# A fifth score buffer in a two-layer graph network: queries wait in DRAM, and U2 takes U1's place

## The chip, the cores and the metric

The kernel runs on one core of a Trainium2 chip. A core has a matrix engine (TensorE, PE in the profile, with its weight loads as PEld), three engines for elementwise work (VectorE or DVE, ScalarE or ACT, GpSimd or POOL), and SyncE (SP), which in this kernel issues nearly all DMA transfers. Each engine takes its instructions in the order in which the program has them and waits where one isn't ready. The metric is the device time of one execution in microseconds.

## The reference

A layer of graph diffusion with a sparsified attention is followed by a graph attention layer; N = 3327 nodes, 256 features. Cut to what is computed:

```python
h = relu(layernorm(x))
# layer 0: two steps
R = adj + I;  R = R / R.sum(-1)
Z = 0; Xf = Xa = h
for n in range(2):
    q = Xa @ W1.T @ W2.T                  # (N, 64)
    k = Xa @ W3.T                         # (N, 64)
    A = softmax(q @ k.T)                  # (N, N)
    A = A where it is in the row's smallest set that sums to 0.9, else 0
    A = A / A.sum(-1)
    Xf = R @ Xf
    Xa = A @ Xa
    Z = Z + Xf @ U1[n].T + Xa @ U2[n].T
x = x + layernorm(h + Z)
# layer 1: four heads of 64
h = relu(layernorm(x)); hp = h @ W
s, d = hp . a_src, hp . a_dst             # per node and head
P = softmax over j of leaky_relu(s_i + d_j, 0.2) where adj > 0
x = x + elu(P @ hp)
```

Everything is float32. The output is x.

## The kernel before

Nodes are cut into 26 row tiles of 128 (the last has 127). The whole work is one function, `fast`; another, `general`, takes over only for data on which a guess in it fails.

**A plan sets the order.** The class `Plan` collects pieces of work. Each is put with an engine (or two that it may choose between), an estimated length, a rank, the pieces that it needs, a lag after which others may count on it, and the buffers that it takes and gives back, by name. `Plan.order` then simulates a list schedule with these figures: whenever an engine is free, it takes the piece of lowest rank whose needs and buffers are there. The result is a fixed order on each engine, which `Plan.issue` writes out. The figures thus set the order, not the times. Buffers are named there with counts, e.g. four `e`, four `at`, two `pl`, three `et`.

**The start.** Each tile of x is normalised, turned, and projected with `wqk` to a 128-row `kq`, with the key in one half of the partitions and the query in the other (`prepare`, L1212). GpSimd copies the key into `kt`, which holds all keys, and the query into `qq`, which holds all queries (26 x 128 floats in each partition); SP copies the query into the other half of `qq` (`double`, L1246), since the key tiles are spread over both halves[...]. `project_u` (L1263) multiplies each tile with U1 of both steps at once; R is applied to these products afterwards. U1 is in a buffer called `late`, U2 in one of its own; both come in at the start (U2 at 15 us, L584 in the trace). After `project_u`, `late` is used for the weights of layer 1.

**A row tile of a step** (class `Row`):

- logits (L898): PE multiplies the tile's queries with all keys, into 3327 columns, four parts of up to 1024 columns; ACT copies each part to `e`, with the exponential (L913). `e` has 128 x 3328 floats, and there are four such buffers.
- the search for the threshold at which the kept set sums to 0.9: a first guess from the mean and variance of the row's logits (`stats`, L809, from the queries and a sum over the keys, `gk`), counts on ACT (L950), windows and maxima on DVE (L1006, L1011), sorting and choosing on DVE and POOL.
- drop (L1064): DVE sets to zero what is under the threshold, in four parts.
- the turn of the kept probabilities, as PE needs them with columns on partitions. In step 0, three of the four parts go without PE: DVE transposes small blocks in place (`turn_blocks`, L1100), SP writes them to DRAM (`put_blocks`, L1104) and fetches them back in the right order, in four transfers a part (`get_blocks`, L1108); `attend_blocks` (L1118) multiplies them with the features from `e` itself, and only then the buffer is free. The last part, and in step 1 all of them, are turned by PE (L1077) and copied to `et` (L1088); `attend` (L1095).

**Beside it** goes R times the features (class `Full`, L1142): the adjacency is streamed from DRAM in transfers of four tiles (`at`, L1136, seven for a row tile). PE puts such rows between the pieces of the attention.

**The end of a row tile of step 0** (`finish1`, L1280): the attended features are turned, projected to the next step's `kq` (L1299), and multiplied with U2. Before the last logits of step 0, `kt` and `qq` still hold that step's keys and queries; so the new key and query go to DRAM (`spread`, L1311: the key to `kts`, the query to both halves of `qqs`, three transfers); for the last three tiles, which come after those logits, directly to `kt` and `qq`. `fetch_keys` and `fetch_queries` bring them back in two and three large transfers at the turn of the steps. `finish2` (L1376) ends a row of step 1: layer norm, residual and the projections for layer 1.

**Layer 1** (`attend_neighbours`, L1598) runs in four blocks of columns; four of its large tiles lie where the `e` buffers were.

Three parts of the order matter here. All of SP's transfers share one queue of issue: loads of adjacency, puts, gets, the spread of keys and queries, stores. The planner puts row tiles' logits as early as an `e` is free. And the statistics of a step come in three groups of row tiles (0 to 2, 3 to 12, 13 to 25).

Of the kernel before, what the change touches and what calls it, by code (L numbers as in the profile page):

```python
# [19 lines left out]
P = 128  # L20
# [567 lines left out]
def fast(  # L588
# [31 lines left out]
    kts = spill.tile([P, NT * P], F32, name="kts")  # L620
    qqs = spill.tile([P, NT, P], F32, name="qqs")
# [26 lines left out]
    with ExitStack() as l0:  # L648
# [17 lines left out]
        qq = wpool.tile([P, NT, P], F32, name="qq")  # L666

# [5 lines left out]
        u2 = wpool.tile([P, 2, 2 * D], F32, name="u2")  # L673
# [3 lines left out]
        gk = wpool.tile([P, 2 * DA + 1], F32, name="gk")  # L677
        GP.memset(gk, 0.0)
        GP.tensor_copy(gk[:DA, DA + 1 :], ident[:DA, :DA])
# [22 lines left out]
        def weights():  # L702
# [10 lines left out]
            for n in range(STEPS):  # L713
                cols = slice((1 - n) * D, (2 - n) * D)
                uloads.append(
                    plan.put(
                        "SP", 0.4, -196.5 + n, nc.sync.dma_start, u1[:, :, cols],
                        u1t[n].rearrange("(c p) o -> p c o", p=P), lag=8.0,
                    )
                )  # L720
                plan.put(
                    "SP", 0.4, -150.0, nc.sync.dma_start, u2[:, :, cols], u2t[n].rearrange("(c p) o -> p c o", p=P)
                )
# [25 lines left out]

        def layer1_loads():  # L750
# [24 lines left out]
        def moments(t, kq, ps_k, ps_g):  # L775
# [4 lines left out]
            held = {}  # L780
# [28 lines left out]
        def stats(lo, hi, rank, needs, scaled):  # L809
# [6 lines left out]
            def product(held, t0, m):  # L816

                held["ps"] = ps_x.tile([P, 3, 2 * DA + 1], F32, name="px")
                for k in range(m):
                    T.matmul(held["ps"][:, k, :], qq[:, t0 + k, :], gk, start=True, stop=True)  # L820
# [6 lines left out]
            def square(held, t0, m):  # L827
                qg = held["qg"]
                for k in range(m):
                    junk = small.tile([P, DA], F32, name="qj", bufs=1)  # L830
                    V.scalar_tensor_tensor(
                        junk, qg[:, k, :DA], 1.0, qg[:, k, DA + 1 :], ALU.mult, ALU.mult,
                        accum_out=stat[:, 0, t0 + k : t0 + k + 1],
                    )
                V.tensor_copy(stat[:, 1, t0 : t0 + m], qg[:, :m, DA])

            for t0 in range(lo, hi, 3):
                held, m = {}, min(3, hi - t0)
# [24 lines left out]
            return plan.put("DVE", 0.6, rank, rest, needs=[a])  # L863

        plan = Plan(dict(rows=1, mvs=3, pl=2, px=2, acca=1, accf=1, et=3, at=4, y=1, e2=3, mask=2, **BUFS))

        class Row:
# [10 lines left out]
            def open(self):  # L878
                self.e = epool.tile([P, NP], F32, name="e")
# [6 lines left out]
            def logits(self, k):  # L886
# [7 lines left out]
                for r in range(2):  # L894
# [5 lines left out]
                        qq[half, self.i, :],  # L900
# [223 lines left out]
        JC = 4  # L1124

# [52 lines left out]
        def keys_summed(t, kq, ps_k, ps_g, rank, needs, tags, give):  # L1178
            turn, copy, product, gather = moments(t, kq, ps_k, ps_g)
# [32 lines left out]
        def prepare(t, measured):  # L1212
# [28 lines left out]
            def keys():  # L1241
                GP.tensor_copy(kt[mine, cols], held["kq"][mine])
                GP.tensor_copy(qq[other, t, :], held["kq"][other])

            def double():
                nc.sync.dma_start(qq[mine, t, :], held["kq"][other])  # L1246
# [7 lines left out]
            k = plan.put("POOL", 0.7, r, keys, needs=[a])  # L1254
            q = plan.put("SP", 0.2, r, double, needs=[a])
            g = t % 4 == 0 and keys_summed(
                t, lambda: held["kq"], lambda: ps_a.tile([P, P], F32, name="acca"),
# [3 lines left out]
            return [k, q], g  # L1261
# [18 lines left out]
        def finish1(row, done, rank):  # L1280
# [27 lines left out]
            def queries():  # L1308
                GP.tensor_copy(qq[other, t, :], held["kq"][other])

            def spread():  # L1311
                kq = held["kq"]
                if not direct:
                    nc.sync.dma_start(kts[mine, cols], kq[mine])
                    nc.sync.dma_start(qqs[other, t, :], kq[other])
                nc.sync.dma_start((qq if direct else qqs)[mine, t, :], kq[other])

            def project_u2():
                ps = held["pu"] = ps_x.tile([P, 2 * D], F32, name="px")
                for k in range(2):  # L1320
                    T.matmul(ps, held["xt"][:, k, :], u2[:, k, :], start=(k == 0), stop=(k == 1))
# [23 lines left out]
            kq = [a]  # L1345
            if direct:
                kq = [
                    plan.put("DVE", 0.2, r, keys, needs=[a, drawn[0]]),
                    plan.put("POOL", 0.4, r, queries, needs=[a, drawn[0]]),
                ]  # L1350
            kq.append(plan.put("SP", 0.3, r, spread, needs=[a, drawn[0] if direct else None]))
            g = t % 4 == 0 and keys_summed(
                t, lambda: held["kq"], lambda: ps_x.tile([P, P], F32, name="px"),
                lambda: ps_x.tile([P, DA + 1], F32, name="px"), r, [a, guessed[0]], ("px", "px"), [],
            ) or None
            plan.put("SP", 0.02, r, lambda: None, needs=[kq, g], give=["kq"], lag=0.0)
            a = plan.put("PE", 1.75, r + 0.1, project_u2, needs=[x_], take=["px"])
            a = plan.put("ACT", 0.56, r + 0.1, stage, needs=[a], take=["ystage"], give=["px", "xt"])
            a = plan.put("POOL", 0.8, r + 0.3, add, needs=[a])
            y = plan.put("SP", 0.1, r + 0.3, store, needs=[a], give=["ystage"], lag=3.0)  # L1360
            return kq, g, y

        def fetch_keys(r):
            half = slice(r * DA, r * DA + DA)
            w = max(half_of(t)[2].stop for t in range(LAST + 1) if side(t) == r)
            nc.sync.dma_start(kt[half, :w], kts[half, :w])

        def fetch_queries(lo, hi):
            nc.sync.dma_start(qq[:, lo:hi, :], qqs[:, lo:hi, :])
# [6 lines left out]
        def finish2(row, done, z, rank):  # L1376
# [64 lines left out]
            x_ = plan.put("SP", 0.1, r - 1.5, fetch, needs=[row.pieces["guess"]], take=["ystage"], lag=3.0)  # L1441
# [4 lines left out]
            s_ = plan.put("SP", 0.1, r, store, needs=[a])  # L1446
# [35 lines left out]
        def search(row, rank, keys, stats_of, fresh):  # L1482
# [4 lines left out]
            for g in range(2):  # L1487

                def logits(g=g):
# [4 lines left out]
                    "PE", 1.95 - 0.67 * g, rank - 2.5, logits, needs=[keys, fresh, a], take=["pl", "pl"] + ["e", "sc"] * (1 - g)  # L1494
# [37 lines left out]
        GROUPS = -(-NT // 4)  # L1532

        def attention(row, rank, total, drops, right):
            a = None
            if row.i < BLOCKED[row.n]:
                come = []
                for g in range(3):
                    b = plan.put("DVE", 1.25, rank - 1.001, row.turn_blocks, g, needs=[drops[g]])
                    b = plan.put("SP", 0.5, rank - 1.0, row.put_blocks, g, needs=[b], lag=3.5)  # L1540
                    b = plan.put("POOL", 0.02, -90.0, lambda: None, needs=[b], lag=0.0)
                    come.append(
                        [plan.put("SP", 0.45, rank - 1.0, row.get_blocks, g, o, needs=[b], lag=3.5) for o in range(4)]
# [6 lines left out]
                for j in (0, 4, 8, 12, 24, 16, 20):  # L1550
                    if j == 24:
# [4 lines left out]
                        take=["acca"] * (j == 0), give=["e"] * (j == 20),  # L1556
                    )
                return plan.put("ACT", 0.4, rank - 2.7, row.attended, needs=[a, total], take=["xa"], give=["acca", "sc"])
            for g in range(GROUPS):
# [4 lines left out]
                    give=["e"] * (g == GROUPS - 1),  # L1564
# [10 lines left out]
        def full(n, t, rank, right, after):  # L1575
# [3 lines left out]
                plan.put("SP", 0.1, rank, f.load, q, needs=[after], take=["at"], lag=3.3) for q in range(-(-NT // JC))  # L1579
# [13 lines left out]
            if n == 1:  # L1593
                b = plan.put("SP", 0.1, rank, f.fetch, needs=[loads[-1], stored[t]], take=["base"], lag=3.0)
# [3 lines left out]
        def attend_neighbours(rows, ends, done, fulls):  # L1598
# [29 lines left out]
            opened = [plan.put("SP", 0.02, 59.0, open_heads, needs=[logits_done, counted], lag=0.0)]  # L1628
# [48 lines left out]
            for b in range(4):  # L1677
# [14 lines left out]
                for j in range(NT):  # L1692
# [83 lines left out]
                    else:  # L1776
                        loads = [
                            plan.put("SP", 0.1, rank, load, g, needs=[logits_done], take=["at"], lag=4.0)
# [138 lines left out]
        late, hs, turned_h, drawn, guessed, loaded, stored = {}, [[None] * NT], [None] * NT, [None], [None], [None], [None] * NT  # L1917
# [24 lines left out]
        keys, sums = [a for a, _ in parts], [b for _, b in parts]  # L1942
        layer1_ready = None
        sources = [project_u(t, -1.9 + 0.001 * t) for t in range(NT)]
        right, fresh, failed, queries = None, None, [], [None] * NT
        for n in range(STEPS):
# [3 lines left out]
                lambda: V.tensor_scalar(gk[:, : DA + 1], gk[:, : DA + 1], 1.0 / (-(-NT // 4) * P), None, ALU.mult), needs=[sums],  # L1950
            )
            cuts = (0, 3, NT // 2, NT)
            of = {}
            for k in range(3):
                p = stats(
                    cuts[k], cuts[k + 1], base + (-50.0, -2.35, 0.0)[k], [keys, queries[cuts[k] : cuts[k + 1]], fresh],
                    scaled,
                )
                of.update(dict.fromkeys(range(cuts[k], cuts[k + 1]), p))
            if n == 0:  # L1960
                guessed[0] = [*{id(p): p for p in of.values()}.values()]
            rows = [Row(n, i) for i in range(NT)]
            found = [search(r, base + r.i, [keys, queries[r.i]], of[r.i], fresh) for r in rows]
# [8 lines left out]
            if n == 0:  # L1972
                ends = [finish1(r, done[r.i], base + r.i + 0.2) for r in rows]
                stored = [y for _, _, y in ends]

                keys, queries, after = [k for k, _, _ in ends], [k for k, _, _ in ends], [drawn[0]]
                for fn, args, rest in (
                    (fetch_keys, (0,), ends[: LAST + 1]), (fetch_keys, (1,), ends[: LAST + 1]),
                    *((fetch_queries, (lo, min(lo + 8, LAST + 1)), ends[lo : lo + 8]) for lo in range(0, LAST + 1, 8)),
                ):  # L1980
                    p = plan.put("SP", 0.1, base + NT, fn, *args, needs=[after, [k for k, _, _ in rest]], lag=5.0)
                    if fn is fetch_keys:
                        keys.append(p)
                    else:
                        for t in range(*args):
                            queries[t] = [queries[t], p]
                    after = [plan.put("POOL", 0.02, -90.0, lambda: None, needs=[p], lag=0.0)]
                sums = [g for _, g, _ in ends]
# [14 lines left out]
                a = plan.put("SP", 0.5, base + 4.0, layer1, needs=[used, done[3]], take=["et"], lag=8.0)  # L2003
# [79 lines left out]
```

## Time and profile before

| | |
|---|---|
| median of 3 runs | 2159.17 us (2158.55 to 2160.39) |
| the profiled execution | 2158.39 us |
| its span | 2156.6 us |
| granted TensorE clock | 0.995 |
| PE busy | 2098.1 us (97%) |
| weight loads busy | 1464.1 us (68%) |
| DVE busy | 1757.0 us (81%) |
| ACT busy | 1324.9 us (61%) |
| POOL busy | 945.9 us (44%) |
| data moved | 265.5 MB, 123 GB/s on average |

The stages in the trace: the start to about 100 us, step 0 to about 850, step 1 to about 1600, layer 1 to the end. The profile is one execution, so its times differ a little from the median. A line of the table of waits has the engine and what it was to do, what it waited for, then the microseconds in total, the number of waits and the longest. In the timeline a line begins with its start and its length in us; in brackets is the idle time before it and what ended it.

### The profile page before, as it was taken

Reading aid. Unit: us, or ns where it says so; the run is one execution under the profiler, and the core shown is the slowest. Engines: PE = TensorE matmul, PEld = TensorE weight load, DVE = VectorE, ACT = ScalarE, POOL = GpSimd, SP = SyncE. Lnnn points to the kernel's source line nnn. Section 1 sums busy time; section 2 is a strip of 40 time slices with the busy share of each in tenths; the row PEclk is TensorE's granted clock in tenths of the full one; section 3 lists DMA queues with packets and bytes.
Section 4 is the critical chain, followed back from the end, with each engine's and each line's share of the span. In section 5 each row is a group of like instructions: output and inputs, shape, how many; then the busy total and the mean of one; then the engine's idle time right before and its main releaser. Section 6 shows DMA issues by size and latency. Waiting matters only on the chain. (4 is left out here: it accounts for less than half of the span.)

```text
span 2156.6 us, 35324 instructions
## 1 busy us (share of the span) xinstructions
PE 2098.1 (97%) x11247; PEld 1464.1 (68%) x11247; DVE 1757.0 (81%) x4436; ACT 1324.9 (61%) x2444; POOL 945.9 (44%) x2259
## 2 busy tenths in 40 slices
PE   8999999999999999999999999999999999999997
PEld 6577777777777777778877888888888433333332
DVE  5579887878777781578999899978878999989895
ACT  4677565665456621687777767777773556565552
POOL 5367555555554630367667666567553100000001
PEclk9999999999999999999999999999999999999999
DMA  4077777777776796522222222222224545354441
GB/s 122 22 172 186 184 181 177 177 177 173 187 173 162 154 240 181 150 62 76 65 64 59 62 62 62 74 76 75 68 70 134 153 128 160 114 153 117 117 124 33
DMA packets 398243, 265.52 MB, mean 123 GB/s; under 512 B 181370, under 2 KB 352096, under 8 KB 398048
## 3 DMA queue, kind: packets, MB, share of 16 engines
q1 hardware_dynamic: 397152, 262.97, 47.1%
q8 instruction: 91, 1.49, 0.3%
q14 instruction: 104, 0.85, 0.1%
q10 hardware_dynamic: 896, 0.21, 0.0%
HBM read 205.31 MB, written 56.84 MB: 122 GB/s over the span
## 5 line engine op out<-in xcount | busy, mean ns | idle before, releaser
L950 ACT ACTIVATE junk<-e,sc 128x3327 fp8e5<-128x3327 f32 x182 | 558.2, 3067 | 65.2 <-POOL sc L995 64.0
L1095 PE MATMUL acca<-rhs,et 128*128 128x256 f32 x1456 | 336.4, 379 | 0.0
L1142 PE MATMUL accf<-main,at 128*128 128x257 f32 x1352 | 314.0, 383 | 8.3 <-DMA at<-in_adjt_dram 6.6
L1142 PE MATMUL accf<-c,at 128*128 128x256 f32 x1352 | 313.4, 382 | 3.5 <-DVE f L1154 2.5
L1118 PE MATMUL acca<-rhs,e 128*128 128x256 f32 x1248 | 284.6, 383 | 22.3 <-DMA e<-blocks 21.5
L1095 PEld LDWEIGHTS acca<-rhs,et 128*128 128x128 f32 x1456 | 268.9, 190 | 32.3
L1142 PEld LDWEIGHTS accf<-main,at 128*128 128x128 f32 x1352 | 252.0, 190 | 57.0 <-issue 10.9
L1142 PEld LDWEIGHTS accf<-c,at 128*128 128x128 f32 x1352 | 249.8, 190 | 49.1 <-issue 9.7
L1118 PEld LDWEIGHTS acca<-rhs,e 128*128 128x128 f32 x1248 | 243.8, 197 | 57.5 <-issue 23.6
L1006 DVE SCALAR_TENSOR_TENSOR y<-e,sc 128x1639 f32<-128x1639 f32 x104 | 208.6, 2006 | 58.2 <-POOL sc L992 55.9
L1011 DVE MAX8 cands<-y 128x8 f32<-128x205 f32 (+1 forms) x832 | 243.0, 362 | 3.6
L913 ACT ACTIVATE e<-pl 128x1024 f32<-128x1024 f32 x208 | 183.7, 889 | 68.4 <-PE pl L898 66.2
L1064 DVE SCALAR_TENSOR_TENSOR e<-e,thr 128x1024 f32<-128x1024 f32 x208 | 219.0, 1075 | 4.8 <-DVE thr L1059 2.8
L1888 POOL TENSOR_TENSOR qq<-qq 128x256 f32<-128x256 f32 x4 | 3.0, 756 | 446.3 <-ACT qq L1884 446.2
L1722 ACT ACTIVATE et<-at 128x448 bf16<-128x448 f32 (+1 forms) x204 | 112.2, 550 | 130.1 <-DVE e L1733 75.1
L1749 PE MATMUL pl<-e,main 128*64 128x416 f32 x1024 | 188.8, 516 | 0.0
L898 PE MATMUL pl<-kt,qq 64*128 64x512 f32 (+1 forms) x832 | 173.6, 535 | 0.0
L1749 PEld LDWEIGHTS pl<-e,main 128*64 128x64 f32 x1024 | 70.0, 137 | 109.4 <-issue 92.3
L1733 DVE SCALAR_TENSOR_TENSOR e<-c,low,et 128x832 f32<-128x832 f32 x128 | 128.9, 1072 | 6.3 <-issue 3.2
L898 PEld LDWEIGHTS pl<-kt,qq 64*128 64x128 f32 x832 | 71.5, 186 | 83.8 <-issue 75.7
L1721 ACT ACTIVATE at<-at 128x448 f32<-128x448 f32 (+1 forms) x204 | 110.5, 542 | 26.2 <-DMA at<-in_adjt_dram 26.2
L1088 ACT COPY et<-px 128x512 f32<-128x512 f32 (+1 forms) x129 | 67.3, 533 | 95.1 <-PE px L1077 47.8
(546 smaller groups left out, 3408.8 us busy)
## 6 DMA issues: line engine op xcount, KB each, us to landing
at<-in_adjt_dram SPq DMA_DIRECT2D x414, 256.0 KB
blocks<-e SPq DMA_DIRECT2D x78, 512.0 KB
e<-blocks SPq DMA_DIRECT2D x312, 128.0 KB
at<-in_adjt_dram SPq DMA_DIRECT2D x102, 192.0 KB
at<-in_adjt_dram SPq DMA_DIRECT2D x52, 128.0 KB
ys<-ystage SPq DMA_DIRECT2D x26, 256.0 KB
rhs<-in_x_dram SPq DMA_DIRECT2D x26, 128.0 KB
ystage<-in_x_dram SPq DMA_DIRECT2D x26, 128.0 KB
```

The source lines that it names most:

```text
L898: T.matmul(pl[:, lo : lo + m], qq[half, self.i, :], kt[half, 512 * k : 512 * k + m], start=True, stop=True,)
L913: S.activation(to, pl, AF.Exp, accum_out=(self.p0, self.p1, self.p2, self.p3)[k],)
L950: S.activation(junk[:, :N], self.e[:, :N], fn, bias=t, scale=-1.0, accum_out=dst, saturate=False)
L1006: V.scalar_tensor_tensor(self.y[:, : hi - lo], self.e[:, lo:hi], self.up, self.e[:, lo:hi], ALU.is_lt, ALU.mult, accum_out=(self.h0, self. ...
L1011: V.max(self.cands[:, a * PIECES // 2 + k, :], self.y[:, at[k] - lo : at[k + 1] - lo])
L1064: V.scalar_tensor_tensor(piece, piece, self.thr[:, o : o + 1], piece, ALU.is_gt, ALU.mult)
L1095: T.matmul(self.acc, et[:, j - 4 * g, :], rhs[self.n][:, j, :], start=(j == 0), stop=j == NT - 1 and self.i >= BLOCKED[self.n],)
L1118: T.matmul(self.acc, lhs, rhs[self.n][:, j, :], start=(j == 0), stop=stop and j == js[-1])
L1142: T.matmul(self.acc[:, : self.w], self.at[j // JC][:, j % JC, :], self.src[:, j, : self.w], start=(j == 0), stop=(j == NT - 1),)
L1722: S.activation(to, src, AF.Sign)
L1733: V.scalar_tensor_tensor(held["e"][:, k, :], extra["both"][b % 2][:, k, :], low[:, j, k : k + 1], held["mask"], ALU.max, ALU.mult,)
L1749: T.matmul(q["acc"][a][k * FH : (k + 1) * FH, c, :C], main[:, j, h * FH : (h + 1) * FH], held["e"][:, h, c * C : (c + 1) * C], start=(j == 0),
```

## The change

A fifth buffer for `e` is made from the place of `qq`. Of a step's row tiles every fifth (2, 7, 12, 17, 22 in step 0; 1, 6, 11, 16, 21 in step 1) uses it, as `own_e` says; the others share the four.

- *Queries.* They wait in DRAM (`kqs`, one for each step) and come to the chip for four row tiles at a time, into `qg`, of which there are two. Step 0's first eight tiles go there directly, the others by `fetch_queries`: two transfers of 64x512, four small ones for the last group. A group's fetch waits until the logits and statistics that used its buffer are done.
- *Keys and queries of the next step.* `spread` is one transfer of 128x128 for a row tile, `kq` as it is, in place of three. The keys come back in six transfers (64x512 or 64x384) in place of two. GpSimd's copies of queries remain for the first eight tiles alone; the last three tiles of step 0 send their query through DRAM too.
- *U2* is loaded into U1's buffer after the last `project_u`. The weights of layer 1, which take that buffer next, are loaded after the last U2 product has been stored, at the turn of the steps, and layer 1's score products follow there; before, they came at about 220 to 250 us.
- *Statistics* come in groups of four row tiles, in pieces of two instead of three; each step has its own `gk`, so that the next step's key sums needn't wait for this step's statistics.
- *The planner's figures*: lengths of SP's issues go from 0.1 to 0.4 us or so, the lag of a put from 3.5 to 6.0, that of a get from 3.5 to 4.5.

Which matmuls there are isn't changed. The diff, cut:

```diff
-        kts = spill.tile([P, NT * P], F32, name="kts")
-        qqs = spill.tile([P, NT, P], F32, name="qqs")
+        kqs = [spill.tile([P, NT, P], F32, name=f"kqs{n}") for n in range(STEPS)]
...
-        qq = wpool.tile([P, NT, P], F32, name="qq")
...
-        u2 = wpool.tile([P, 2, 2 * D], F32, name="u2")
...
-        gk = wpool.tile([P, 2 * DA + 1], F32, name="gk")
+        gks = [wpool.tile([P, 2 * DA + 1], F32, name=f"gk{n}") for n in range(STEPS)]
...
-                plan.put(
-                    "SP", 0.4, -150.0, nc.sync.dma_start, u2[:, :, cols], u2t[n].rearrange("(c p) o -> p c o", p=P)
-                )
...
+        def u2_loads():
+            late["u2"] = wpool.tile([P, 2, 2 * D], F32, name="late")
+            for n in range(STEPS):
+                nc.sync.dma_start(
+                    late["u2"][:, :, (1 - n) * D : (2 - n) * D], u2t[n].rearrange("(c p) o -> p c o", p=P)
+                )
...
-            for t0 in range(lo, hi, 3):
-                held, m = {}, min(3, hi - t0)
+            for t0 in range(lo, hi, 2):
+                held, m = {}, min(2, hi - t0)
...
+        own_e = [[("e", "e5")[i % 5 == 2 - n] for i in range(NT)] for n in range(STEPS)]
...
-                self.e = epool.tile([P, NP], F32, name="e")
+                if own_e[self.n][self.i] == "e":
+                    self.e = epool.tile([P, NP], F32, name="e")
+                else:
+                    self.e = wpool.tile([P, NP], F32, name="qq")
...
-                GP.tensor_copy(qq[other, t, :], held["kq"][other])
+                if t < 8:
+                    if t % 4 == 0:
+                        qg[0, t // 4] = small.tile([P, 4, P], F32, name="qg", bufs=2)
+                    GP.tensor_copy(qg[0, t // 4][other, t % 4, :], held["kq"][other])
 
             def double():
-                nc.sync.dma_start(qq[mine, t, :], held["kq"][other])
+                to = qg[0, t // 4][mine, t % 4, :] if t < 8 else kqs[0][other, t, :]
+                nc.sync.dma_start(to, held["kq"][other])
...
+        def fetch_queries(n, g):
+            lo, hi = 4 * g, min(4 * g + 4, NT)
+            to = qg[n, g] = small.tile([P, 4, P], F32, name="qg", bufs=2)
+            for t0, t1 in ((lo, hi),) if g < 6 else ((24, 25), (25, 26)):
+                other = half_of(t0)[1]
+                for r in range(2):
+                    nc.sync.dma_start(to[r * DA : r * DA + DA, t0 - lo : t1 - lo, :], kqs[n][other, t0:t1, :])
...
             def spread():
-                kq = held["kq"]
-                if not direct:
-                    nc.sync.dma_start(kts[mine, cols], kq[mine])
-                    nc.sync.dma_start(qqs[other, t, :], kq[other])
-                nc.sync.dma_start((qq if direct else qqs)[mine, t, :], kq[other])
+                nc.sync.dma_start(kqs[1][:, t, :], held["kq"])
...
-                    b = plan.put("SP", 0.5, rank - 1.0, row.put_blocks, g, needs=[b], lag=3.5)
+                    b = plan.put("SP", 0.5, rank - 1.0, row.put_blocks, g, needs=[b], lag=6.0)
...
-                        [plan.put("SP", 0.45, rank - 1.0, row.get_blocks, g, o, needs=[b], lag=3.5) for o in range(4)]
+                        [plan.put("SP", 0.6, rank - 1.0, row.get_blocks, g, o, needs=[b], lag=4.5) for o in range(4)]
...
-                plan.put("SP", 0.1, rank, f.load, q, needs=[after], take=["at"], lag=3.3) for q in range(-(-NT // JC))
+                plan.put("SP", 0.4, rank, f.load, q, needs=[after], take=["at"], lag=3.3) for q in range(-(-NT // JC))
...
+        u2_loaded = plan.put("SP", 0.9, -1.7, u2_loads, needs=sources, lag=5.0)
...
-            cuts = (0, 3, NT // 2, NT)
...
+            for g in range(GROUPS):
+                lo, hi = 4 * g, min(4 * g + 4, NT)
+                r = base + lo - 6.0
+                if n == 0 and g < 2:
+                    q = saved[lo:hi]
+                else:
+                    q = plan.put(
+                        "SP", 1.2, r, fetch_queries, n, g, needs=[saved[lo:hi], all_saved if n == 0 else None], take=["qg"], lag=3.0
+                    )
+                known, read = stats(n, lo, hi, base - 50.0 if g == 0 else r, [keys, q, fresh], scaled)
+                found += [search(rows[t], base + t, [keys, q], known, fresh) for t in range(lo, hi)]
...
-                a = plan.put("SP", 0.5, base + 4.0, layer1, needs=[used, done[3]], take=["et"], lag=8.0)
+                a = plan.put("SP", 1.8, base + NT + 1.0, layer1, needs=[used, stored], take=["et"], lag=8.0)
```

## The prediction

> **What bounds the kernel now.** I read the page's busy times first, then TensorE's waits, then the engines by stretch, then the timeline around the longest wait.
>
> ```profile
> PE 2098.1 (97%) x11247; PEld 1464.1 (68%) x11247; DVE 1757.0 (81%) x4436; ACT 1324.9 (61%) x2444; POOL 945.9 (44%) x2259
> ```
>
> TensorE (PE) works 2098.1 of the span's 2156.6 us, so 58.5 us are all that a new order can win. The table of stretches (columns: length, then PE, weight loads, DVE, ACT and POOL busy, granted clock, DMA share, GB/s) says where they lie:
>
> ```profile
> 0.00:60.00 60.00, 50.91 (x286) 37.99 (x287) 30.24 (x121) 30.43 (x83) 32.00 (x111) 0.94 0.39 111
> 60.00:100.00 40.00, 39.98 (x117) 17.98 (x116) 21.80 (x83) 25.46 (x60) 14.00 (x40) 1.00 0.00 1
> 100.00:850.00 750.00, 718.38 (x3285) 567.06 (x3285) 575.80 (x1526) 427.15 (x723) 400.28 (x956) 1.00 0.76 179
> 850.00:1600.00 750.00, 745.20 (x3769) 604.03 (x3766) 629.54 (x2011) 550.64 (x911) 458.88 (x1072) 1.00 0.27 76
> 1600.00:2157.00 557.00, 543.66 (x3801) 237.03 (x3799) 499.65 (x698) 291.20 (x670) 40.72 (x82) 0.99 0.41 121
> ```
>
> Idle PE: 9.1 us at the head, 31.6 in step 0 (100 to 850 us), 4.8 in step 1, 13.3 after, of which some 12 are the tail after the last matmul. Step 0 holds more than half, and TensorE's waits name its cause:
>
> ```profile
> PE acca L1118 <- DMA e<-blocks: 21.5, 16, 3.1
> PE accf L1142 <- DMA at<-in_adjt_dram: 6.6, 5, 2.9
> PE px L1233 <- ACT kq L1239: 4.2, 2, 3.1
> ```
>
> Here the first product of a row tile's attention (L1118) waits for the gathers of that row's transposed blocks (21.5 us in 16 waits). The longest one in the timeline:
>
> ```profile
> 227.74 2.51 SPq L1111 DMA_DIRECT2D e<-blocks  x4
> ...
> 229.82 1.03 PE L1095 MATMUL acca<-rhs,et 128*128 128x256 f32 x4
> 233.91 3.73 PE L1118 MATMUL acca<-rhs,e 128*128 128x256 f32 x16 [3.06 <-DMA e<-blocks]
> ```
>
> The last gather is issued by 230.25 and PE goes on 3.7 us later, so the row itself is late. From a step-0 row's first logits (L898) to its first L1118 the shortest chains of the trace take 66 us (row 0 66.1, row 21 66.0, row 19 66.3, row 20 66.7). Between those two points the order puts other PE work; multiplying each instruction by its duration in the trace (0.432 us a 128x256 pair, 3.35 us a row's logits, 1.72 us a U2 product), that is 71.8 us on average, and the rows that wait are those with 62 to 68.
>
> **What the Trainium skill says.** "Perfetto Trace Analysis", Optimization Strategy: consistent bubbles can mean that there isn't room for the next tile, i.e. too few buffers. The trace agrees in part: a row of step 0 takes PE about 28.7 us (750 over 26), four e buffers thus span 115 us, and the chain (66), the attention and the waiting in between have to fit in them. "DMA: Bandwidth & Descriptors", Anatomy of one DMA: a transfer costs some 2 us whatever its size, mostly its completion, and a semaphore wait stands on the issuing sequencer before dispatch. The trace agrees: the 3.7 us above, for 128 KB. It also means that a load which waits holds up whatever is behind it on SP. Same page, Issuing engines are not separate DMA queues: small transfers are bound by their descriptors. The trace has 181370 of 398243 packets under 512 bytes, mostly these gathers; their number doesn't change.
>
> **The change part by part**, against the profiled execution's 2158.39 us (1.8 outside the span; the median of the runs is 0.8 higher, which I add at the end). No matmul is added or removed; in the changed program PE has the same instructions in another order. So everything is idle time.
>
> 1. *Fifth e buffer and the new planner lags in step 0.* Counted the same way in the changed order, 83.8 us of PE work lie between a row's first logits and its first L1118, 12 more than before. The rows at or under the 66 us chain are 0 (62.6), 1 (64.7), 12 (64.5) and 13 (65.9); the next are 14 (70.6) and 20 (71.2). Row 12 waits about 1.7, row 13 about 0.3, row 1 nothing, as row 0's wait comes in between. About 2 more for chains that run longer than the shortest. With row 0 (next step, 4.1) some 8 of 21.5 us remain: **-13.4**.
> 2. *U2's load.* Before, U1 and U2 were both on chip by 16 us. Now U2 goes into U1's buffer, so its two loads wait on SP for the last `project_u`, and the first adjacency loads stand behind them. Those were fetched far ahead:
>
> ```profile
> 49.41 2.00 SPq L1136 DMA_DIRECT2D at<-in_adjt_dram  x4
> ```
>
>    That cover is gone: two issues at 0.47 us, one of 0.5, then 768 KB at the 330 GB/s of those four loads (1 MB from 50.8 to 54.0 us; 2.3 us for 768 KB) and completion, about 4 us; PE has 2.0 us of logits to do meanwhile, so it stops for some 2 us (1.5 to 4) near 100 us. The same time counts for row 0's chain: its turn stands 53.4 us of PE work after its logits, and took 57.0. Both together cost 4.1 us in place of 1.55, which is in step 1's remainder.
> 3. *The head.* U2's two loads (0.94 us of SP, 512 KB, 1.6 us at 330 GB/s) no longer stand in front of the queries' copies at 15.2 us. PE's stop of 3.13 us before 21.18 is on that path: **-1.7** (0 to -2.5).
> 4. *Step 0 to step 1.* The first row of step 1 has its turn 60.5 us of PE work after its first logits (64.7 before). Before, that chain took 65.0 us, 2.9 of it behind statistics on DVE that now come elsewhere: 62.1, so **+1.5** (0 to 5). The next have 66, 76 and 75.5. Layer 1's score products (eight DVE operations of 0.42 us at 247 us) move here, where DVE waits for rows anyway; its cost without that cover is 3.4. The keys' fetch, six transfers instead of two, is 2 us of SP; row 24, the first behind it, has 81.7 us for its 66.
> 5. *Fewer transfers, more of others.* A row's key and query leave in one issue instead of three (0.46 to 0.93 us each), 46 fewer; 22 fetches of queries and keys come in place of 5. SP's issues for a row were 12 x 0.51, 3 x 0.39, 7 x 0.33 and about 2 more, 11.5 of 28.7 us: not a bound. 0 on the path, and a little for the gathers behind them. The fetches wait on SP for logits that are four or more rows old: 0, if those are done by then.
> 6. *Statistics in seven groups instead of three*: four more times seven small DVE operations a step (L844 to L858, 0.17 us each) and three more copies (L835, 0.17), 5.3 us a step. DVE works 575.8 of 750 and 629.5 of 750: hidden, but where it stands in a chain it shows: **+1** (0 to 3).
> 7. Adjacency waits (6.6 us), step 1's other rows (PE work from logits to turn 84.6 before, 85.5 after, none under 73), layer 1 and the tail: unchanged, **0** (-6 to +8 for the adjacency loads, which share SP's queue with a new order).
>
> Sum: -13.4 - 1.7 + 1.5 + 1 = -12.6; 2158.4 - 12.6 + 0.8 = 2146.6, about 2147.
>
> **Rivals.**
> *More is won.* If the 4 idle us of row 0 overlap and the new order also ends the adjacency waits and the rest of the row waits, -21.5 + 4.1 - 1.7 - 6.6 = -25.7: 2133. For it: those waits come from the same queue, now less loaded. Against: they are five single events (at 302, 331, 566, 762 and 798 us), and the puts and gathers that they share SP with all stay.
> *The place is taken.* The longer distance is used up: chains get longer because an earlier row means more rows in flight on DVE and ACT, or because a put waits on SP for its transposition. The mean real chain was already 76, against the shortest of 66; if it went to 84 to 88, the waits come back to 18 or so: about 2156. Against: DVE and ACT are at 77% and 57% in step 0, and a row may sit ready without harm.
> *Slower: adjacency loads behind waiting puts.* SP keeps its order. Puts and gathers now stand further ahead of their use, so SP may wait for DVE's transpositions while adjacency loads stand behind them with only four buffers' lead (16 matmuls, 7 us). At 0.9 us of late loads for each of 26 rows, +23, the result is -12.6 + 23 = +10: 2170. It turns the sign from 0.5 us a row (12.6 / 26), and reaches the slower side from 0.65. For it: five such waits exist already, up to 2.9 us. Against: they were 0.25 us a row.
>
> **How the numbers follow.** Chances: the forecast 0.50, more won 0.20, place taken 0.15, slower 0.15. A difference under 0.2% (4.3 us) is about what a measurement of this kernel can't tell from none. The forecast and the first rival lie below 2154.9; of the place taken a fifth does, the rest is the same: faster 0.73, same 0.12, slower 0.15. For 8 in 10 the range goes from 2136 (the sum with steps 1, 3 and 7 at their good ends) to 2164 (place taken whole and the beginning of the slower case); the forecast's own range is 2140 to 2153.
>
> **What would show it.** Right: waits of L1118 for blocks of 5 to 10 us in all, among them row 0, 12 and 13; PE idle 15 to 24 us between 100 and 850 us instead of 31.6; a stop near 100 us before the first L1142; a gap of under 2 us where 3.13 stood; a first turn of step 1 late by 0 to 3. Wrong: waits of L1118 of 15 us or more with longer chains (place taken), L1142 waiting for `at` over 20 us (slower), or more than 5 us of new idle time in step 1, where I see nothing change.

## The result, and the profile after

The kernel after takes 2145.39 us (median of 4 runs, 2141.34 to 2147.9), the kernel before 2159.12 us (median of 4, run with it); the ratio is 0.9934, 95% interval 0.9917 to 0.9951. The forecast was 2147 with a range of 2136 to 2164.

The profiled execution took 2146.1 us, its span is 2144.3 us. First the page's busy times and the table of stretches of the kernel after (columns as before):

```profile
PE 2096.3 (98%) x11247; PEld 1467.9 (68%) x11247; DVE 1763.6 (82%) x4510; ACT 1319.7 (62%) x2446; POOL 960.8 (45%) x2248
```

```profile
0.00:60.00 60.00, 52.12 (x282) 37.33 (x283) 30.53 (x116) 29.40 (x81) 26.32 (x95) 0.94 0.31 84
60.00:100.00 40.00, 35.76 (x100) 15.40 (x99) 19.11 (x66) 27.66 (x62) 14.67 (x39) 1.00 0.12 38
100.00:850.00 750.00, 739.14 (x3400) 587.87 (x3399) 581.93 (x1595) 427.87 (x740) 420.27 (x961) 0.99 0.79 184
850.00:1600.00 750.00, 740.87 (x3753) 603.55 (x3752) 647.29 (x2086) 559.10 (x917) 475.40 (x1113) 1.00 0.26 73
```

PE's idle time went from 58.5 to 48.0 us (2144.3 - 2096.3). By stretch: head 9.1 to 7.9, 60 to 100 us nothing to 4.2, step 0 from 31.6 to 10.9, step 1 from 4.8 to 9.1; what is left, after 1600 us, from 12.9 to 15.9. So step 0 won 20.7 us, and the change lost about half of that again elsewhere. TensorE's waits, from the top of the kernel after's answer and then the two lines on the blocks (those rows whose e lies in the fifth buffer read `qq`):

```profile
PE accf L1150 <- DMA at<-in_adjt_dram: 8.3, 3, 3.8
PE accf L1150 <- DVE f L1162: 4.2, 3, 1.7
PE accf L1150 <- ACT f L1157: 3.9, 3, 3.3
...
PE acca L1125 <- DMA qq<-blocks: 0.8, 2, 0.5
...
PE acca L1125 <- DMA e<-blocks: 0.3, 1, 0.3
```

The waits for blocks fell from 21.5 us to 1.1. The largest stops now are others. In the timeline of the kernel after, the first is U2's, the second comes with layer 1's weights, which SP issues after the first fetch of features and ahead of the next adjacency loads:

```profile
99.66 8.00 PE L1150 MATMUL accf<-main,at 128*128 128x257 f32 x28 [3.84 <-DMA at<-in_adjt_dram]
```

```profile
814.12 0.43 SPq L1383 DMA_DIRECT2D rhs<-ys  x1
814.59 0.68 SPq L757 DMA_DIRECT2D late<-in_ln_g_dram  x1
815.32 0.48 SPq L758 DMA_DIRECT2D late<-in_ln_b_dram  x1
815.84 0.43 SPq L759 DMA_DIRECT2D et<-in_gat_a_dram  x1
816.31 0.43 SPq L760 DMA_DIRECT2D late<-in_gat_w_dram  x1
816.84 4.15 SPq L1144 DMA_DIRECT2D at<-in_adjt_dram  x4
```

```profile
781.91 0.41 PE L1084 MATMUL px<-ident,e 128*128 128x128 f32 x2 [2.09 <-DVE bad L1474]
...
824.26 4.45 PE L1150 MATMUL accf<-main,at 128*128 128x257 f32 x12 [3.62 <-DMA at<-in_adjt_dram]
...
933.83 2.50 PE L1150 MATMUL accf<-c,at 128*128 128x256 f32 x5 [3.25 <-ACT f L1157]
```

### The profile page after: what moved, and what is told of

It is laid out like the page before. It is cut to its first block, busy times and chain, and to the rows that moved or that the text cites. A ratio compares the mean times of both kernels' runs of the same rounds, so it can differ in the third digit from the quotient of the medians.

```text
span 2144.3 us, 35321 instructions
## 1 busy us (share of the span) xinstructions
PE 2096.3 (98%) x11247; PEld 1467.9 (68%) x11247; DVE 1763.6 (82%) x4510; ACT 1319.7 (62%) x2446; POOL 960.8 (45%) x2248
## 5 line engine op out<-in xcount | busy, mean ns | idle before, releaser
L957 ACT ACTIVATE junk<-e,sc 128x3327 fp8e5<-128x3327 f32 x147 | 450.8, 3066 | 53.6 <-POOL sc L1002 52.5
L1125 PE MATMUL acca<-rhs,e 128*128 128x256 f32 x1008 | 226.1, 380 | 0.3 <-DMA e<-blocks 0.3
L1125 PEld LDWEIGHTS acca<-rhs,e 128*128 128x128 f32 x1008 | 196.7, 196 | 24.3 <-issue 2.4
L1013 DVE SCALAR_TENSOR_TENSOR y<-e,sc 128x1639 f32<-128x1639 f32 x84 | 166.3, 1980 | 36.4 <-POOL sc L999 35.0
L1071 DVE SCALAR_TENSOR_TENSOR e<-e,thr 128x1024 f32<-128x1024 f32 (+1 forms) x168 | 176.5, 1073 | 3.4 <-DVE thr L1066 1.4
L905 PE MATMUL pl<-kt,qg 64*128 64x512 f32 (+1 forms) x832 | 173.5, 535 | 0.0
L920 ACT ACTIVATE e<-pl 128x1024 f32<-128x1024 f32 (+1 forms) x168 | 148.0, 890 | 36.9 <-PE pl L905 35.5
L905 PEld LDWEIGHTS pl<-kt,qg 64*128 64x128 f32 x832 | 71.6, 186 | 81.7 <-issue 71.9
```

The source lines that it names most:

```text
L905: T.matmul(pl[:, lo : lo + m], qg[self.n, self.i // 4][half, self.i % 4, :], kt[half, 512 * k : 512 * k + m], start=True, stop=True,)
L920: S.activation(to, pl, AF.Exp, accum_out=(self.p0, self.p1, self.p2, self.p3)[k],)
L957: S.activation(junk[:, :N], self.e[:, :N], fn, bias=t, scale=-1.0, accum_out=dst, saturate=False)
L1013: V.scalar_tensor_tensor(self.y[:, : hi - lo], self.e[:, lo:hi], self.up, self.e[:, lo:hi], ALU.is_lt, ALU.mult, accum_out=(self.h0, self. ...
L1071: V.scalar_tensor_tensor(piece, piece, self.thr[:, o : o + 1], piece, ALU.is_gt, ALU.mult)
L1125: T.matmul(self.acc, lhs, rhs[self.n][:, j, :], start=(j == 0), stop=stop and j == js[-1])
```

## The experiments

The prediction put the fifth buffer and the planner's new lags into one step. The first question is which of the two did it.

**The lags alone, and all but the lags.** Theory A: the lags make the room between a row's logits and its products. Theory B: the fifth buffer does. `before_new_lags` is the kernel before with

```diff
-                    b = plan.put("SP", 0.5, rank - 1.0, row.put_blocks, g, needs=[b], lag=3.5)
+                    b = plan.put("SP", 0.5, rank - 1.0, row.put_blocks, g, needs=[b], lag=6.0)
-                        [plan.put("SP", 0.45, rank - 1.0, row.get_blocks, g, o, needs=[b], lag=3.5) for o in range(4)]
+                        [plan.put("SP", 0.6, rank - 1.0, row.get_blocks, g, o, needs=[b], lag=4.5) for o in range(4)]
```

> The kernel before with four e buffers, all queries on chip and U2 loaded early, and only the planner's figures for a put (lag 6.0 in place of 3.5) and a get (0.6 and 4.5 in place of 0.45 and 3.5) of the kernel after. Theory A, the figures make the room: in the order that they give, 82.5 us of PE work lie between a step-0 row's first logits and its first L1118 (71.8 before, 83.8 after), so the waits for blocks fall from 21.5 us to 5 or less, nothing is lost to U2's load, and the time is 2135 to 2145. Theory B, the fifth buffer makes the room: with four buffers the rows can't be opened early enough, waits for blocks or for e of 15 us or more stay, and the time is 2153 to 2160.

`after_old_lags` is the kernel after with the reverse of this diff.

> The kernel after with those same figures of the planner put back to 3.5, 0.45 and 3.5; the fifth buffer and all else stay. Theory A: the order leaves only 75.4 us of PE work, and ten or so rows have under 66, so waits for blocks of 15 to 25 us come back and the time is 2158 to 2170. Theory B: the buffer is still there, the waits stay under 8 us and the time is 2143 to 2150.

`after_four_e` is the kernel after with

```diff
-        own_e = [[("e", "e5")[i % 5 == 2 - n] for i in range(NT)] for n in range(STEPS)]
+        own_e = [["e"] * NT for n in range(STEPS)]
```

> The kernel after with every row in the four e buffers; the fifth lies unused. Theory A: the order still leaves 79.6 us of PE work, rows 0, 1 and 20 are the only ones under 66, waits for blocks are 2 to 6 us and the time is 2143 to 2152. Theory B: waits for blocks of 15 us or more and 2157 or more.

Measured, as ratios to the kernel before on the same chip: the lags alone 0.9922 (0.9905 to 0.9938), 2137.8 us; all but the lags 1.0061 (1.0044 to 1.0078), 2168.4 us; all with four buffers 0.9944 (0.9927 to 0.9961), 2143.6 us. The lines on the blocks in the waits of these three, in this order (the second has one for rows in `e` and one for rows in `qq`):

```profile
PE acca L1118 <- DMA e<-blocks: 4.4, 5, 1.9
```

```profile
PE acca L1125 <- DMA e<-blocks: 15.6, 14, 2.3
...
PE acca L1125 <- DMA qq<-blocks: 1.0, 1, 1.0
```

```profile
PE acca L1125 <- DMA e<-blocks: 3.7, 5, 1.3
```

A holds and B falls. Three numbers in the plan (the two lags and the length of a get), without any new buffer, win as much as the whole change (the intervals overlap). With the old numbers the change is slower than the kernel before. With the new ones the fifth buffer is worth nothing that can be seen (0.9944 without, 0.9934 with, each uncertain by 0.0017). Two things are open. With the old numbers the waits for blocks still fell from 21.5 us to 16.6, and what the buffer has in that was not tried by itself. Nor was it tried which of the three numbers brings the gain.

For the get, the trace of before shows that the figure was too low: in the 11 rows of step 0 whose first L1118 stops over 0.3 us, it begins 2.8 to 4.8 us after the last gather of its first part was issued, median 4.2. The plan counted 3.5 and so put the product where the data weren't yet; 4.5 is short in three of the 11 rows only, and there by 0.3 us at most. For the put no such comparison was made.

Not every wait comes from there. The longest of before (3.06 us at 233.91, shown in the prediction) is at the third part of row 4, and it begins 3.7 us after its last gather was issued, so it is the issue that is late. These gathers stand on SP behind layer 1's four loads, at their old place:

```profile
221.15 0.75 SPq L756 DMA_DIRECT2D late<-in_ln_g_dram  x1
221.94 0.43 SPq L757 DMA_DIRECT2D late<-in_ln_b_dram  x1
222.41 0.43 SPq L758 DMA_DIRECT2D et<-in_gat_a_dram  x1
222.89 0.43 SPq L759 DMA_DIRECT2D late<-in_gat_w_dram  x1
```

Row 4 waits in four of the five kernels that load them there (3.06, 0.82, 6.32 and 1.53 us), and hardly in those that load them later (0.31 us at most). So it is likely that moving these loads also took a wait away; it wasn't tried by itself.

**The two stops that the change brought.** `after_at_first` plans the first row's adjacency loads after eight of the products with U1; so four of them stand before U2's on SP:

```diff
-                full(n, t, (min(1.0 + 1.15 * t, 27.0) if n == 0 else base + 1.0 + t), [p[0] for p in sources], [p[1] for p in sources] if n == 0 else loaded[0])
+                full(n, t, (min(1.0 + 1.15 * t, 27.0) if n == 0 else base + 1.0 + t), [p[0] for p in sources], ([p[1] for p in sources[: 26 if t else 8]]) if n == 0 else loaded[0])
```

> The kernel after with the first row's adjacency loads planned after eight of the first products with U1 instead of all, which puts four of these loads ahead of U2's on SP; the rest of the order moves with it. If U2's place at the head of SP's queue is what stops PE at 99.7 us, that stop (3.84 us) goes to under 1 us and the time is 2 to 4 us under that of the kernel after, unless row 0's chain then shows at its first L1118 (65.2 us of PE work in this order: up to 2 us). If the stop is due to something else (the DMA engines busy with U2 itself), 2 us or more of it stay.

The stop of 3.84 us became one of 1.11 (for DVE), so its cause was U2's place on SP. But the time is 2144.2 us, ratio 0.9950 (0.9933 to 0.9966), no gain where 2 to 4 us were expected: the order of everything behind it moved, and a stop that was not there before stands at 489 us.

```profile
489.28 0.89 PE L1150 MATMUL accf<-main,at 128*128 128x257 f32 x3 [2.83 <-issue]
```

`after_l1_later` holds layer 1's weights back by 110 us of the plan:

```diff
+                slow = plan.put("POOL", 0.02, -90.0, lambda: None, needs=[stored], lag=110.0)
-                a = plan.put("SP", 1.8, base + NT + 1.0, layer1, needs=[used, stored], take=["et"], lag=8.0)
+                a = plan.put("SP", 1.8, base + NT + 1.0, layer1, needs=[used, slow], take=["et"], lag=8.0)
```

> The kernel after with layer 1's weights planned 110 us later, in step 1; the order of step 0 up to there is the same. If those loads, ahead of the adjacency's on SP and the DMA engines, cause the stop of 3.62 us at 824 us, it goes to under 1 us and with the slow clock that follows it (1.7 us) the time falls by 3 to 6 us. If the fetch of the features (512 KB each) does it, 2 us or more of the stop stay and the time is the same within 2 us.

2134.2 us, ratio 0.9891 (0.987 to 0.9911), against 0.9934: 9 us, more than expected, and that with a stop at 98 us that is longer here (4.88 us). The stop at 824 us is gone, as these lines of its timeline show (no bracket), and so are those at 934 and 1617 us:

```profile
814.74 7.33 PE L1150 MATMUL accf<-main,at 128*128 128x257 f32 x33
822.00 1.99 PE L905 MATMUL pl<-kt,qg 64*128 64x512 f32 x8
823.92 11.35 PE L1150 MATMUL accf<-main,at 128*128 128x257 f32 x51
```

So the loads, not the features' fetch, made the adjacency late. That the two later stops came from the score products which follow those loads on DVE is likely, as these moved with them; it wasn't tried apart.

`after_both` has both edits.

> The kernel after with both: the first row's adjacency loads ahead of U2's, and layer 1's weights later. If the two stops at 100 and 824 us are independent costs that the change brought, the sum of the two gains, 2137 to 2141 against 2145.4 of the kernel after. If a stop that is taken away only moves on, 2143 or more.

2132.4 us, 0.9886 (0.9866 to 0.9907): below the range expected, but not to be told from `after_l1_later`. Beside the second edit, too, the first gives no gain that can be seen.

**The transfers.** `after_three_spreads` sends a row's key and query out in three transfers again, two of them to where nobody reads:

```diff
                 nc.sync.dma_start(kqs[1][:, t, :], held["kq"])
+                nc.sync.dma_start(extra_kq[mine, t, :], held["kq"][mine])
+                nc.sync.dma_start(extra_kq[other, t, :], held["kq"][other])
```

> The kernel after with two more transfers a row tile where the key and query leave (64x128 each, to a buffer in DRAM that nobody reads): three as in the kernel before, the plan unchanged. If the number of these transfers is off the critical path, the time is that of the kernel after, plus 0 to 2 us. If fewer issues on SP carry part of the gain, gathers and adjacency loads come later, waits for them grow by 5 us or more and the time by as much.

2144.9 us, 0.9944 (0.9925 to 0.9963), where the kernel after has 0.9934: off the path.

**U2 at the head.** `before_u2_late` is the kernel before with U2 still in its own buffer, loaded when the queries' copies are through; `before_lags_u2_late` has the new lags as well.

```diff
-                plan.put(
-                    "SP", 0.4, -150.0, nc.sync.dma_start, u2[:, :, cols], u2t[n].rearrange("(c p) o -> p c o", p=P)
-                )
...
         keys, sums = [a for a, _ in parts], [b for _, b in parts]
+        for n in range(STEPS):
+            plan.put(
+                "SP", 0.45, -1.7, nc.sync.dma_start, u2[:, :, (1 - n) * D : (2 - n) * D],
+                u2t[n].rearrange("(c p) o -> p c o", p=P), needs=[keys],
+            )
```

> The kernel before with its own figures for puts and gets, and only U2's loads (own buffer) moved behind the queries' copies. By itself this takes away the stop of 3.1 us at 21 us and, with the slow clock after it, 3 to 5 us. Its order also changes: 74.1 us of PE work before the first L1118 on average, and the rows under 66 us lack 12.5 us together (28.6 before), so waits for blocks of 8 to 14 us are left of 21.5. Theory that both effects add up: 2140 to 2148. Theory that the gain of before_lags_u2_late needs the new lags: 2150 or more, with waits for blocks of 18 us or more.

> The kernel before with the new lags for puts and gets (as in before_new_lags), and U2, still in its own buffer, loaded after the queries' copies instead of at 15 us. If U2's load is what makes PE stop for 2.8 us at 20.6 us, that stop shrinks by 1 to 2 us, nothing stops near 100 us for U2 (its buffer is free, so SP doesn't wait), and the time is 1 to 4 us under that of before_new_lags, if the rest of the order stays as good (81.1 us of PE work before the first L1118, row 0 with 62.3 the only one clearly under 66: up to 3 us for it). If the queries' copies themselves are the cause, the stop stays at 2.5 us or more.

With the old lags it wins nothing: 2159.2 us, 1.0009 (0.9996 to 1.0022). The head's idle time did fall, from 9.1 to 4.8 us (60 less 55.16 busy), and the waits for blocks took it back:

```profile
PE acca L1115 <- DMA e<-blocks: 28.5, 22, 6.3
```

The order count had let me expect 8 to 14 us of such waits; one of the 22 alone is 6.3, again at row 4 behind layer 1's loads. With the new lags the same edit gives 2126.5 us, 0.9857 (0.9839 to 0.9876), against 0.9922 without it: 14 us by the ratios, where 1 to 4 were expected, with 6.3 us of waits for blocks left. So the theory that it needs the lags held. The head shows 2.5 of the 14 (PE busy 53.92 of the first 60 us, 51.40 without the edit), and a stop of 4.1 us at 151 us is gone, too; where the rest comes from isn't settled.

**More lag, and the fifth buffer once more.** `before_longer_put_u2_late` has the put's lag at 9.5:

```diff
-                    b = plan.put("SP", 0.5, rank - 1.0, row.put_blocks, g, needs=[b], lag=6.0)
+                    b = plan.put("SP", 0.5, rank - 1.0, row.put_blocks, g, needs=[b], lag=9.5)
```

> As before_lags_u2_late, with the put's lag at 9.5 instead of 6.0. In the order that this gives, 86.2 us of PE work lie between first logits and first L1118, and no row has under 70. If the distance is what decides, the waits for blocks (6.3 us in before_lags_u2_late) go under 1 us and the time falls to 2119 to 2125; if such rows only push the wait elsewhere, 2126 or more.

2122.4 us, 0.9835 (0.9811 to 0.9859), the lowest time here, though its interval overlaps with that of the shorter lag (0.9857). It is 1.65% under before and 1% under after by the ratios, with four e buffers, all queries on chip and none of the change's other edits. Its busy times and the line on the blocks:

```profile
PE 2090.1 (99%) x11247; PEld 1460.3 (69%) x11247; DVE 1760.4 (83%) x4451; ACT 1318.7 (62%) x2429; POOL 964.9 (46%) x2259
```

```profile
PE acca L1115 <- DMA e<-blocks: 4.7, 7, 1.5
```

The time is as expected, but 4.7 us of waits for blocks are left where I had said under 1, though in its trace, too, every row has over 70 us of PE work before its first product. So the distance alone doesn't decide. What shows in PE's gaps is that no stop between the head and the tail is longer than 1.6 us any more.

`after_both_longer_put` is `after_both` with that lag, `after_both_longer_put_four_e` the same with four buffers.

> The kernel of after_both (five e buffers) with the put's lag at 9.5 instead of 6.0: 83.4 us of PE work before the first L1118, no row under 67.5. after_both has hardly any waits for blocks left (under 1 us), so a longer lag has nothing to win: the same within 3 us, 2129 to 2136. If it still wins 4 us or more, what these lags do is more than the blocks' waits.

> The same with every row in the four e buffers, the fifth unused: 83.6 us of PE work, no row under 68. If the fifth buffer gives nothing in this schedule, the time is that of after_both_longer_put within 3 us. If the fifth buffer carries a part of the change's gain, it is 5 us or more longer, with waits of ACT or PE for an e buffer.

2126.8 us, 0.9853 (0.9829 to 0.9877), with five buffers, and 2124.5 us, 0.9844 (0.9821 to 0.9868), with four; neither has a wait for blocks. The fifth buffer gives nothing here either. But with the longer lag the time is some 6 us under `after_both` (0.9853 against 0.9886, whose intervals just overlap), which had no wait for blocks to lose. That is below the range that I gave; if the gain is real, the figures change more than those waits. PE's gaps say what: the stops of 2.8 us at 491 us and of 1.9 at 743 are gone; they were at products with R (one near 140 us grew from 1.6 to 2.1).

## Why the prediction was right or wrong

The sum was -12.6 us and the profiled executions differ by 12.3. That it fits so well is chance: its terms were off in both directions. Two of the prediction's own signs of being right did not come: it wanted 5 to 10 us of waits for blocks (1.1 are left) and 15 to 24 us of idle PE between 100 and 850 us (10.9).

- *Step 1, -13.4 for the waits for blocks: the direction right, the size too small, the reason right in part.* They fell by 20.4. PE work between logits and product grew as counted (71.8 and 83.8; the real time was 75.7 and 85.2 us on average). The 2 us for longer chains and row 0's wait at its first product didn't come. But this distance doesn't say which rows wait. Of the 11 first products that wait in before, four are in rows with 75 to 86 us of PE work (rows 3, 10, 18 and 23, 6.0 of some 15 us), and row 1 went on after 60.5 us without waiting, so 66 wasn't the shortest chain. In the kernel after, four rows have 65 to 67 us, and of these only row 12 waits at its first product (0.5 us). But the step named the buffer and the lags together, and read the bubbles, with the Trainium skill's "Perfetto Trace Analysis" (Optimization Strategy), as a sign of too few buffers. The runs showed that the planner's figures do it alone; four buffers were enough.
- *Step 2, U2's load: the place and the mechanism right.* I said a stop of some 2 us (1.5 to 4) near 100 us before the first product with R, 4.1 with row 0's chain; it is 3.84, all at the loads, with row 0's product not late after it. What I left out is the clock that follows (below): these 28 matmuls took 8.00 us, where 28 took 6.25 elsewhere, 1.75 more. The 2 us that the prediction gives for any transfer is, in the Trainium skill's "DMA: Bandwidth & Descriptors" (Anatomy of one DMA), a figure for transfers that GpSimd issues; these come from SP, and a gather of 128 KB was used 2.8 to 4.8 us after its issue.
- *Step 3, the head, -1.7:* the stop of 3.13 us became 1.32, the head as a whole gave 1.2.
- *Step 4, the turn of the steps, +1.5: the step that failed.* I looked for a wait of step 1's first row, which isn't there. I had priced the moved load of layer 1 by its DVE products alone, not by its four DMA issues and the data on the way to them, which stand ahead of the adjacency loads there: 3.62 us at 824 us. The drop and transposition of step 0's last row end late on DVE, 2.09 at 782 (the line names DVE's next operation; the drop that PE needs ends at 781.76). Together with the stop at 934 us that is 9.0 us and the slow clock after each. Undoing the one load alone gave 9 us back, although the stop at 782 stays there (1.96 us) and so isn't the load's.
- *Step 5 (transfers), 0:* right for the key and query that leave, as shown by `after_three_spreads`. The count of fetches was not: the trace has 28 of queries and 6 of keys, not 22 in all.
- *Step 6, DVE +5 us a step:* DVE worked 6.6 us more in all; whether the +1 shows anywhere wasn't tried.
- *Step 7, adjacency waits 0, range -6 to +8:* without the stops of steps 2 and 4, 0.8 us of 6.6 are left, so -5.8. Step 1 of the diffusion I had unchanged; it lost 4.3 us. The tail after the last matmul, which I had read as some 12 us before, was 10.6.

The first rival (more won) was right on the waits: `after_both`, in which the stop at 824 us is gone and the one near 100 us is down to 1.12, took 2132.4 us against its 2133. The slower rival, late adjacency loads behind waiting puts, didn't happen; late adjacency loads behind other loads did. The rival by which the place of the blocks' waits is taken by longer chains is wrong for the kernel after; `before_u2_late`, where the head's gain went into waits for blocks, comes nearest to it.

## What to carry to other kernels

Where a planner with estimated delays writes a fixed order, compare its delays with the trace before giving it more buffers: here new figures for a put and a get, one of them up to 1.3 us too low for the gathers that stopped PE, won as much as the whole change, and the new buffer nothing beside them. Price a moved load by its issues and its bytes in the queue where it lands, not only by what consumes it. And count a stop of PE of 3 us or more with the slow clock after it.

## What I had not expected of the hardware

A stop of PE can cost more than its length. The 14 traces give the granted clock in the 8 us after every stop of PE over 1 us, head and tail left out. After 85 stops shorter than 1.75 us it was not lower (but for one, which a longer stop follows within these 8 us); after 13 of 27 stops from 1.75 to 3 us and 17 of 19 longer ones it was, mostly 0.79, which is 1.7 us of full speed lost (0.21 of 8). The stretches before, at and after U2's stop in the kernel after (the third last column is the clock):

```profile
91.70:99.70 8.00, 3.94 (x13) 1.44 (x13) 7.76 (x24) 6.40 (x18) 3.35 (x6) 1.00 0.56 179
99.70:107.70 8.00, 8.00 (x30) 6.43 (x31) 7.48 (x23) 5.76 (x6) 3.90 (x10) 0.79 0.36 101
120.00:128.00 8.00, 8.00 (x39) 7.22 (x38) 6.88 (x15) 5.71 (x8) 4.43 (x11) 1.00 1.17 219
```

The Trainium skill, "TensorE: Matmul & The Clock Gate", in the section on HAM oscillation, gives the rule to leave no idle gap of PE over some 3.4 us. The runs agree for the long ones and show that about half of those from 1.75 to 3 us count as well; what decides among these isn't settled. It can explain a part of why `before_longer_put_u2_late` has 2090.1 us of busy PE where before has 2098.1, for the same matmuls, at a mean clock of 0.998 against 0.995.
